# Triangle layer: normalising the input and filling the first channel quarter in one interleaved loop instead of two loops one after the other

## The chip, the cores and the metric

One core of one Trainium2 chip runs the kernel. The metric is the device time of one execution in microseconds (us). The engines are named as the profile names them: PE is the matrix engine, PEld its weight load, DVE the vector engine, ACT the engine of activation functions, POOL the general engine that here scales, shifts and issues stores, and SP the queue that issues loads.

## The reference, cut to what matters

A picture of 256 x 256 pixels with 128 channels goes through four layers, each as `x = x + layer(groupnorm(x))`: attention, a recurrence in the frequency domain, a triangle layer, a convolution. Only the triangle layer is touched. In short, in the reference's own names:

```python
pair_norm = layer_norm(pair, ln_in_w, ln_in_b)          # over the 128 channels of a pixel
p = einsum('bijd,hd->bijh', pair_norm, p_in_w)          # 256 channels out
g = sigmoid(einsum('bijd,hd->bijh', pair_norm, g_in_w))
left, right = g[..., :H] * p[..., :H], g[..., H:] * p[..., H:]
out = einsum('bikd,bjkd->bijd', left, right / L)        # for each channel d a 256x256x256 product
out = einsum('bijh,dh->bijd', layer_norm(out, ...), p_out_w)
return sigmoid(einsum('bijd,ed->bije', pair_norm, g_out_w)) * out
```

`pair` is the group-normalised x, that is x times a factor a plus a shift b for each channel.

## The kernel before, in words

The picture lies in DRAM as 128 channels (partitions) by 65,536 pixels, in 32-bit floats: x2T is the layer's input, znT its normalised input, x3T its output. `triangle` works in these stages:

1. `group_affine` (L1145) turns the statistics of the layer before into the columns `ab` (a and b); `centering` (L136) makes `lc`, the 128 x 128 matrix that takes the channel mean away, scaled by a, and `cb`, the centred b.
2. The norm, a loop over 32 blocks of 2,048 pixels (L1190 to L1235). `load` brings a block into `xin` (a pool of three). `centre` multiplies it by `lc`, two products of 512 pixels for each half block into the PSUM tile `zc`, and DVE adds `cb` into `zs`. `square` is ACT's `sq`. `variance` makes the channel mean of `sq` by four products with a weight 32 columns wide, one for each 512 pixels, which land beside each other on the 128 partitions of one bank; ACT takes `Ln` and `Exp` of it (`rs`). `spreads` brings these rows back to 128 partitions, by four products whose contraction is 32 rows (`pr`). DVE multiplies `zs` by `pr` into `zn`, POOL applies weight and bias in place (L1234) and issues the store to znT (L1235).
3. For each of four channel quarters g: the fill, a loop over 64 half blocks (L1246 to L1257), then the products. The fill loads a block of znT back (`zt`, L1249, the same ring of five buffers that held `zn`), makes eight products with 128 pixels as the weight and the quarter's 128 columns of `wf` as the moving side (`z`), takes `Sigmoid` of one half of the columns (`sg`) and multiplies the other half by it into `LR`, which holds the quarter for the whole picture. The products (`po`, L1259 to L1269) read LR across all pixels: none can start before the quarter's last LR column is written.
4. The output loop (from L1275 on), not touched. It has a mean by narrow products too, `mn`, copied by ACT into `mr` and spread by `spreads`, and it changes ACT's table set twice in each block.

Every engine runs its own instructions in order. Most calls in `triangle` are wrapped in `pin`, which keeps them in the order in which the code issues them on their engine. Before the first block, the loads of `xin` for blocks 0 to 2 have been issued at 2955 to 2962 us, long before `ab` is known at 2997.7 us. ACT's functions come in table sets: the norm uses the set of Ln and Exp, the fill that of Sigmoid, so the set was changed once between the two stages (at 3202.62 us).

Of the kernel before, what the change touches and what calls it, by code (L numbers as in the profile page):

```python
# [9 lines left out]
F32 = mybir.dt.float32  # L10
AF = mybir.ActivationFunctionType
ALU = mybir.AluOpType
AX = mybir.AxisListType
PSUM = bass.MemoryType.PSUM
# [3 lines left out]
P = 128  # L18
# [8 lines left out]
LN_EXP = "natural_log_exp_and_others"  # L27
EXP_TANH = "exp_and_others"
SIGMOID = "sigmoid_and_others"


class Kernel:
# [21 lines left out]
    def act(self, out, in_, func, bias=0.0, scale=1.0, **kw):  # L54
        return self.nc.scalar.activation(out, in_, func, bias=bias, scale=scale, **kw)  # L55

    def table(self, name, key="table"):
        return self.chain(key, self.nc.scalar.preload_act_table_set(name))

    def mm(self, out, lhsT, rhs, start=True, stop=True):  # L60
        return self.nc.tensor.matmul(out, lhsT, rhs, start=start, stop=stop)  # L61
# [1067 lines left out]
    def triangle(self, x2T, x3T, znT, prodD, stats2, shift2, stats3, prepare):  # L1129
# [3 lines left out]
        nc, tc, I = self.nc, self.tc, self.i  # L1133
        V = nc.vector
        NB, G, CQ = NPIX // 1024, 4, P // 4
        pin = lambda f: lambda *a, **k: tc.keep_in_program_order(f(*a, **k))  # L1136
        mm, act, copy = pin(self.mm), pin(self.act), pin(nc.scalar.copy)
        tt, ts, stt, bn = pin(V.tensor_tensor), pin(V.tensor_scalar), pin(V.scalar_tensor_tensor), pin(V.bn_stats)
        table, add = pin(nc.scalar.preload_act_table_set), pin(V.tensor_scalar_add)
        flat = lambda t: t.rearrange("p k n -> p (k n)")  # L1140
        MUL, ADD = ALU.mult, ALU.add
        with ExitStack() as c:
            wp = c.enter_context(self.pool(name="tw", bufs=1))
            with self.pool(name="twp", bufs=2, space=PSUM) as ps0:
                ab = self.group_affine(wp, ps0, stats2, self.g4, "2", shift=shift2, busy=11)  # L1145
                lc, cb = self.centering(wp, ps0, ab, "2")
                W = self.weights
                lnw, lnb, low, lob = (W[n] for n in ("in_w", "in_b", "out_w", "out_b"))
                wpg, oraw, we = W, W["o"], W["e"]
                pb = ps0.tile([P, 2], F32, name="tpbo", tag="gn")  # L1150
                self.mm(pb[:, 0:1], oraw, lob)
                wbo = wp.tile([P, 1], F32, name="twbo")
                V.tensor_copy(wbo, pb[:, 0:1])
                wo = wp.tile([P, P], F32, name="two")
                V.tensor_scalar_mul(wo, oraw, low)

                wf = wp.tile([P, G, 4, CQ], F32, name="wf")
                for n, m in enumerate("gp"):
                    for side in range(2):
                        V.tensor_copy(wf[:, :, 2 * n + side, :],  # L1160
                                      wpg[m][:, side * P:(side + 1) * P].rearrange("c (g d) -> c g d", g=G))
# [7 lines left out]
            V.memset(m32, 1.0 / P)  # L1169
            spread = wp.tile([P, P], F32, name="tspread")  # L1170
            V.memset(spread, 1.0 / 32)

            def variance(ps, work, sq):

                var = ps.tile([P, 512], F32, name="var", tag="r", bufs=2)
                for k in range(4):
                    mm(var[32 * k:32 * k + 32], m32, sq[k // 2][:, (k % 2) * 512:(k % 2 + 1) * 512])
                rs = work.tile([P, 512], F32, name="rs")
                act(rs, var, AF.Ln, bias=self.eps)
                act(rs, rs, AF.Exp, scale=-0.5)  # L1180
                return rs

            def spreads(ps, rs):
                pr = [ps.tile([P, 1024], F32, name="pr", tag="w") for _ in range(2)]
                for k in range(4):
                    mm(pr[k // 2][:, (k % 2) * 512:(k % 2 + 1) * 512], spread[32 * k:32 * k + 32], rs[32 * k:32 * k + 32])
                return pr


            with ExitStack() as c1:  # L1190
                io = c1.enter_context(self.pool(name="t1", bufs=3))
                work = c1.enter_context(self.pool(name="t1w", bufs=4))
                ps = c1.enter_context(self.pool(name="t1s", bufs=3, space=PSUM))
                xin, sq, zs = {}, {}, {}

                def load(m):
                    if m < NB // 2:
                        xin[m] = io.tile([P, 2048], F32, name="xin")
                        nc.sync.dma_start(xin[m], x2T[:, m * 2048:(m + 1) * 2048])

                def centre(m, b):
                    if m >= NB // 2:
                        return
                    zc = ps.tile([P, 1024], F32, name="zc", tag="w")
                    for k in range(2):
                        s = b * 1024 + k * 512
                        mm(zc[:, k * 512:(k + 1) * 512], lc, xin[m][:, s:s + 512])
                    zs[m, b] = work.tile([P, 1024], F32, name="zs")
                    add(zs[m, b], zc, cb)

                def square(m, b):
                    if m < NB // 2:
                        sq[m, b] = work.tile([P, 1024], F32, name="sq")
                        act(sq[m, b], zs[m, b], AF.Square)

                table(LN_EXP)
                for m in range(2):
                    load(m)
                for b in range(2):
                    centre(0, b)  # L1220
                    square(0, b)
                for m in range(NB // 2):
                    load(m + 2)
                    centre(m + 1, 0)
                    rs = variance(ps, work, [sq[m, b] for b in range(2)])
                    square(m + 1, 0)
                    centre(m + 1, 1)
                    square(m + 1, 1)
                    pr = spreads(ps, rs)
                    zn = zp.tile([P, 2048], F32, name="zn", tag="zt")  # L1230
                    for b in range(2):
                        z = zn[:, b * 1024:(b + 1) * 1024]
                        tt(z, zs[m, b], pr[b], MUL)
                        nc.gpsimd.tensor_scalar(z, z, lnw, lnb, MUL, ADD)  # L1234
                    nc.gpsimd.dma_start(znT[:, m * 2048:(m + 1) * 2048], zn)  # L1235

            with ExitStack() as c1:

                LR = c1.enter_context(self.pool(name="tl", bufs=1)).tile([P, 2, 2, 2 * CQ, P], F32, name="LR")
                work = c1.enter_context(self.pool(name="t2w", bufs=2))  # L1240
                io = c1.enter_context(self.pool(name="t2", bufs=3))
                ps = c1.enter_context(self.pool(name="t2s", bufs=2, space=PSUM))
                table(SIGMOID)
                for g in range(G):

                    for b in range(NB):  # L1246
                        if b % 2 == 0:
                            zt = zp.tile([P, 2048], F32, name="zt", tag="zt")
                            nc.sync.dma_start(zt, znT[:, b * 1024:(b + 2) * 1024])  # L1249
                        z = ps.tile([P, 8, P], F32, name="z", bufs=3)  # L1250
                        for ch in range(8):
                            o = (b % 2) * 1024 + ch * P
                            mm(z[:, ch, :], zt[:, o:o + P], wf[:, g].rearrange("c t d -> c (t d)"))
                        sg = work.tile([P, 8, 2 * CQ], F32, name="sg")
                        act(sg, z[:, :, :2 * CQ], AF.Sigmoid)
                        rows = lambda t: t.rearrange("p (x q) f -> p x q f", x=2)
                        tt(LR[:, :, :, :, 2 * b:2 * b + 2].rearrange("p a k f x -> p x (a k) f"),  # L1257
                           rows(z[:, :, 2 * CQ:]), rows(sg), MUL)

                    for d in range(CQ):  # L1260
                        po = ps.tile([P, 2, 2, P], F32, name="po")
                        for a in range(2):
                            for kc in range(2):
                                mm(po[:, a], LR[:, a, kc, d, :], LR[:, :, kc, CQ + d, :], start=kc == 0, stop=kc == 1)
                        o = io.tile([P, 2, P, 2], F32, name="o")
                        for a in range(2):
                            act(o[:, a], po[:, a].rearrange("p b j -> p j b"), AF.Copy, scale=1.0 / N)
                        nc.gpsimd.dma_start(prodD[g * CQ + d].rearrange("(p a j) -> p a j", p=P, a=2),  # L1268
                                            o.rearrange("p a j b -> p a (j b)"))  # L1269
# [5 lines left out]
            with ExitStack() as c1:  # L1275
# [3 lines left out]
                M = NB // 2  # L1279
# [370 lines left out]
```

## Time and profile before

| what | value |
| --- | --- |
| median of three runs | 4823.47 us (4823.44 to 4824.69) |
| profiled execution, its own time | 4823.77 us |
| its span | 4821.7 us |
| PE busy over the span | 96% |
| DVE, ACT, POOL busy over the span | 75%, 68%, 42% |
| norm stage, 2998.66 to 3205.17 us | 206.5 us |
| first quarter's fill, 3205.17 to 3324.28 us | 119.1 us |
| first quarter's products, 3324.28 to 3379.80 us | 55.5 us |
| granted PE clock | 0.99 |

The span runs from the first instruction to the last; 2.1 us of the execution's own time lie around it. Times in the text count from the span's start. A row of the timeline gives start, length, engine, line, operation, the tile written and the tiles read, the shape, how many instructions of the kind follow each other, and in brackets the idle time of the engine before it with what ended it. Each 32-bit matmul of the program shows as two instructions, so `x8` is four products. Lengths reach from the start of an instruction to its end; consecutive instructions of an engine overlap by a little, so the distance between two starts is what an engine can repeat.

### The profile page before, as it was taken

To read this page: it belongs to the slowest core of one execution; us is meant where nothing else is said; L and a number is where in the kernel's file an instruction comes from. 1 tells how busy PE (TensorE), PEld (TensorE's weight loads), DVE (VectorE), ACT (ScalarE), POOL (GpSimd) and SP (SyncE) were. 2 spreads that over 40 slices of the span, in tenths; PEclk is the share of its full clock that TensorE was granted. 3 is DMA by queue.
4 is the path that set the end of the run, shared out by engine and by line. 5 is a ranking of instruction groups with operands and counts; after the bars stand their busy time and mean duration, and the time that the engine had idled before them with its cause. 6 is when DMAs were issued, how large, how long until landed. Compare 5 with 4: busy or idle time off the path is not lost.

```text
span 4821.7 us, 78838 instructions
## 1 busy us (share of the span) xinstructions
PE 4634.6 (96%) x30671; PEld 2636.5 (55%) x30671; DVE 3635.7 (75%) x4553; ACT 3288.8 (68%) x4978; POOL 2007.2 (42%) x1356
## 2 busy tenths in 40 slices
PE   8999999999999899999999997999999999999999
PEld 2444555555555433333333332259999943369999
DVE  6676777777777699999999996763533448899886
ACT  6456888888888799999999996543333357752110
POOL 0343555555555366666676664421011024420000
PEclk9999999999999999999999998999999999999999
DMA  8893122222222245555555555996866779954432
GB/s 302 311 350 116 49 84 88 81 84 89 82 83 88 80 101 132 133 132 129 133 133 133 130 134 128 331 329 237 282 226 224 239 299 386 368 216 162 134 120 71
DMA packets 221172, 835.17 MB, mean 173 GB/s; under 512 B 59158, under 2 KB 62508, under 8 KB 172260
## 3 DMA queue, kind: packets, MB, share of 16 engines
q1 hardware_dynamic: 144622, 498.19, 30.4%
q0 software_dynamic: 74880, 331.50, 23.7%
q8 instruction: 246, 4.03, 0.3%
q14 instruction: 128, 1.05, 0.1%
q10 hardware_dynamic: 1296, 0.40, 0.0%
HBM read 497.84 MB, written 265.03 MB: 158 GB/s over the span
## 4 chain that ended last, share of the span: by engine, by line
PE 66%; ACT 15%; DVE 11%; issue 6%; DMA 2%; POOL 1%; SPq 0%; ACTq 0%; DVEq 0%; POOLq 0%
PE z L61 10%; PE m L61 8%; PE nd L61 7%; PE sc L61 6%; PE zc L61 5%; PE po L61 5%; PE ppq L61 3%; PE ppv L61 3%; PE pe L61 2%; PE py L61 2%; PE ppg L61 2%; PE ppk L61 2%; PE px L61 2%; PE var L61 2%; ACT L950 2%
## 5 line engine op out<-in xcount | busy, mean ns | idle before, releaser
L609 DVE TENSOR_TENSOR e<-sc,bT 128x1024 f32<-128x1024 f32 x512 | 613.4, 1219 | 255.9 <-PE sc L61 253.8
L609 POOL TENSOR_TENSOR ks<-e 128x1024 f32<-128x1024 f32 x256 | 601.6, 2367 | 442.5 <-PE nd L61 429.0
L55 ACT ACTIVATE e<-e 128x1024 f32<-128x1024 f32 x512 | 539.7, 1054 | 39.6 <-DVE e L609 29.9
L1136 DVE TENSOR_TENSOR LR<-z,sg 128x512 f32<-128x512 f32 x256 | 268.4, 1048 | 364.4 <-ACT sg L55 364.4
L61 PE MATMUL m<-U,v 128*128 128x128 f32 x4608 | 514.7, 275 | 0.0
L61 PEld LDWEIGHTS m<-U,v 128*128 128x128 f32 x4608 | 514.6, 192 | 0.0
L61 PE MATMUL z<-wf,zt 128*128 128x128 f32 x4096 | 460.9, 276 | 1.4 <-DVE zn L1136 1.4
L61 PEld LDWEIGHTS z<-wf,zt 128*128 128x128 f32 x4096 | 460.7, 193 | 2.4 <-DVE zn L1136 2.2
L55 ACT ACTIVATE sg<-z 128x512 f32<-128x512 f32 x256 | 152.8, 597 | 309.1 <-PE z L61 309.1
L1268 POOL DMA_DIRECT2D prodD<-o x128 | 69.0, 540 | 618.7 <-ACT o L55 608.8
L61 PE MATMUL sc<-proj 32*128 32x256 f32 x4096 | 300.4, 403 | 2.8 <-DVE e L609 1.9
L978 POOL TENSOR_TENSOR fs<-f 128x512 f32<-128x512 f32 x64 | 175.7, 2745 | 270.6 <-DVE f L975 251.0
L61 PEld LDWEIGHTS sc<-proj 32*128 32x128 f32 x4096 | 188.3, 185 | 160.7 <-PE px L61 94.8
L61 PE MATMUL nd<-e,proj 128*32 128x256 f32 x4096 | 272.1, 383 | 2.6 <-DVE og L609 2.6
L55 ACT ACTIVATE dn<-dn 128x512 f32<-128x512 f32 x384 | 237.9, 620 | 10.1 <-DVE dn L609 6.0
L978 POOL TENSOR_TENSOR u<-t,tr 128x512 f32<-128x512 f32 x64 | 235.3, 3676 | 11.1 <-DVE tr L981 10.0
L1136 POOL TENSOR_TENSOR xin<-ga,xin 128x1024 f32<-128x1024 f32 x62 | 145.5, 2363 | 210.2 <-DVE ga L1136 210.2
L978 POOL TENSOR_TENSOR t<-t,v 128x1024 f32<-128x1024 f32 x64 | 209.6, 3275 | 54.4 <-DVE t L975 54.4
L61 PE MATMUL po<-LR 128*128 128x256 f32 x1024 | 222.1, 379 | 6.9 <-DVE LR L1136 6.9
L1526 ACT COPY m4s<-m 128x512 f32<-128x512 f32 x32 | 18.7, 584 | 289.9 <-PE m L61 289.9
L1536 POOL DMA_DIRECT2D out_dram<-ys x32 | 37.0, 1155 | 425.4 <-DVE ys L1534 425.4
L61 PEld LDWEIGHTS po<-LR 128*128 128x128 f32 x1024 | 194.2, 190 | 34.0 <-DVE LR L1136 7.7
(385 smaller groups left out, 10713.1 us busy)
## 6 DMA issues: line engine op xcount, KB each, us to landing
zt<-znT SPq DMA_DIRECT2D x128, 1024.0 KB
xin<-x2T SPq DMA_DIRECT2D x64, 1024.0 KB
znT<-zn POOLq DMA_DIRECT2D x61, 1024.0 KB, 5.2
xin<-in_x_dram SPq DMA_DIRECT2D x48, 1024.0 KB
xr<-x3T SPq DMA_DIRECT2D x46, 768.0 KB
x1T<-x POOLq DMA_DIRECT2D x64, 512.0 KB, 4.9
xf<-x1T SPq DMA_DIRECT2D x64, 512.0 KB
xc<-x1T SPq DMA_DIRECT2D x128, 256.0 KB
```

Of the source, the lines that this page charges most:

```text
L55: return self.nc.scalar.activation(out, in_, func, bias=bias, scale=scale, **kw)
L61: return self.nc.tensor.matmul(out, lhsT, rhs, start=start, stop=stop)
L609: pin = lambda f: lambda *a, **k: tc.keep_in_program_order(f(*a, **k))
L950: pin(nc.scalar.preload_act_table_set(want))
L978: pin(nc.gpsimd.tensor_tensor(out, a, b_, op))
L1136: pin = lambda f: lambda *a, **k: tc.keep_in_program_order(f(*a, **k))
L1268: nc.gpsimd.dma_start(prodD[g * CQ + d].rearrange("(p a j) -> p a j", p=P, a=2), o.rearrange("p a j b -> p a (j b)"))
L1526: nc.scalar.copy(m4, m[4])
L1536: nc.gpsimd.dma_start(out[row:row + 8].rearrange("r p t c -> p (r t) c"), ys.rearrange("p g k t c -> p (g k t) c"))
```

## The change

The norm of all 32 blocks and the fill of quarter 0 become one loop, written as a list of steps with a lag each: in iteration `it` a step with lag l works on block it - l. One tile per block holds the input, then the centred input, then the normalised input (in place, in the ring of five). The mean is no longer taken away by `lc`: a weight 32 columns wide, `m32a`, which is 1/128 times a, makes the mean of a x as `mn`; ACT copies it to `mr`; `spreads` brings it to 128 partitions (`mb`); DVE makes a x minus mean in one instruction (`zs`). `cb` moves into ACT's `Square` as its bias and into DVE's `(x + cb) * pr` (`zn`). The fill reads the tile straight after POOL's weight and bias; quarter 0 reads nothing of znT back. znT is still stored, since quarters 1 to 3 and the output loop read it. The fill works on 512 pixels at a time in one bank (`z`, a ring of two), instead of on 1,024 in two banks (a ring of three). Mean and variance share a ring of two banks, both kinds of spread rows share a ring of two pairs of banks; `mr`, `sq` and `rs` have one buffer each. `tabled` changes ACT's table set wherever the next step needs another. LR's buffer is taken before the loop.

```diff
-                lc, cb = self.centering(wp, ps0, ab, "2")
+                pc = ps0.tile([P, 2], F32, name="pc2", tag="gn")
+                self.mm(pc[:, 0:1], self.cmat, ab[:, 1:2])
+                cb = wp.tile([P, 1], F32, name="cb2")
+                V.tensor_copy(cb, pc[:, 0:1])
...
+            m32a = wp.tile([P, 32], F32, name="tmeana")
+            V.tensor_scalar_mul(m32a, m32, ab[:, 0:1])
...
-                for m in range(NB // 2):
-                    load(m + 2)
-                    centre(m + 1, 0)
-                    rs = variance(ps, work, [sq[m, b] for b in range(2)])
-                    square(m + 1, 0)
-                    centre(m + 1, 1)
-                    square(m + 1, 1)
-                    pr = spreads(ps, rs)
-                    zn = zp.tile([P, 2048], F32, name="zn", tag="zt")
-                    for b in range(2):
-                        z = zn[:, b * 1024:(b + 1) * 1024]
-                        tt(z, zs[m, b], pr[b], MUL)
-                        nc.gpsimd.tensor_scalar(z, z, lnw, lnb, MUL, ADD)
-                    nc.gpsimd.dma_start(znT[:, m * 2048:(m + 1) * 2048], zn)
...
+                    work = c2.enter_context(self.pool(name="t1w", bufs=1))
+                    ps = c2.enter_context(self.pool(name="t1s", bufs=2, space=PSUM))
...
+                    def tabled(name, *a, **k):
+                        if loaded[0] != name:
+                            table(name)
+                            loaded[0] = name
+                        act(*a, **k)
+
+                    def four(d, name, w, srcs):
+                        d[name] = ps.tile([P, 512], F32, name=name, tag="r")
+                        for k in range(4):
+                            mm(d[name][32 * k:32 * k + 32], w, srcs[k])
...
+                    def ld(d):
+                        d["x"] = zp.tile([P, 2048], F32, name="zn", tag="zt")
+                        nc.sync.dma_start(d["x"], x2T[:, d["p"] * 2048:(d["p"] + 1) * 2048])
+                    def mn(d): four(d, "mn", m32a, [chunk(d["x"], k) for k in range(4)])
+                    def mc(d):
+                        d["mr"] = work.tile([P, 512], F32, name="mr")
+                        act(d["mr"], d["mn"], AF.Copy)
+                    def mb(d): d["mb"] = spreads(ps, d["mr"])
+                    def zs(d):
+                        for h in range(2):
+                            stt(half(d["x"], h), half(d["x"], h), ab[:, 0:1], d["mb"][h], MUL, ALU.subtract)
+                    def sq(d):
+                        d["sq"] = work.tile([P, 2048], F32, name="sq")
+                        for h in range(2):
+                            act(half(d["sq"], h), half(d["x"], h), AF.Square, bias=cb)
+                    def vr(d): four(d, "vr", m32, [chunk(d["sq"], k) for k in range(4)])
+                    def rs(d):
+                        d["rs"] = work.tile([P, 512], F32, name="rs")
+                        tabled(LN_EXP, d["rs"], d["vr"], AF.Ln, bias=self.eps)
+                        act(d["rs"], d["rs"], AF.Exp, scale=-0.5)
+                    def pr(d): d["pr"] = spreads(ps, d["rs"])
+                    def zn(d):
+                        for h in range(2):
+                            stt(half(d["x"], h), half(d["x"], h), cb, d["pr"][h], ADD, MUL)
+                    def af(d):
+                        for h in range(2):
+                            pin(nc.gpsimd.tensor_scalar)(half(d["x"], h), half(d["x"], h), lnw, lnb, MUL, ADD)
+                    def sto(d): pin(nc.gpsimd.dma_start)(znT[:, d["p"] * 2048:(d["p"] + 1) * 2048], d["x"])
+                    def fill(k):
+                        def f(d):
+                            d["z", k] = ps.tile([P, 4, P], F32, name="z", tag="z")
+                            for ch in range(4):
+                                o = k * 512 + ch * P
+                                mm(d["z", k][:, ch, :], d["x"][:, o:o + P], wf[:, 0].rearrange("c t d -> c (t d)"))
+                        def s(d):
+                            d["g", k] = work.tile([P, 4, 2 * CQ], F32, name="sg", bufs=2)
+                            tabled(SIGMOID, d["g", k], d["z", k][:, :, :2 * CQ], AF.Sigmoid)
+                        def t(d):
+                            tt(LR[:, :, :, :, 4 * d["p"] + k].rearrange("p a k f -> p (a k) f"), d["z", k][:, :, 2 * CQ:], d["g", k], MUL)
+                        return f, s, t
+                    (f0, s0, t0), (f1, s1, t1), (f2, s2, t2), (f3, s3, t3) = (fill(k) for k in range(4))
+                    order = (
+                     (ld, 0), (mn, 0), (pr, 2), (zn, 2), (af, 2), (f3, 3), (f1, 3), (mc, 0), (s3, 3), (t3, 3),
+                     (s1, 3), (vr, 1), (t1, 3), (mb, 0), (f0, 2), (rs, 1), (f2, 2), (s2, 2), (zs, 0), (s0, 2),
+                     (t0, 2), (sq, 0), (sto, 2), (t2, 2),
+                    )
+                    for it in range(M + max(lag for _, lag in order)):
+                        for step, lag in order:
+                            if 0 <= it - lag < M:
+                                D[it - lag]["p"] = it - lag
+                                step(D[it - lag])
...
-                    for b in range(NB):
+                    for b in range(NB if g else 0):
```

More of the change, by code (lines that the diff above doesn't have):

```diff
@@ L1190, in triangle @@
             with ExitStack() as c1:
[L1191 to L1214, printed above, removed]
@@ L1216, in triangle @@
-                table(LN_EXP)
-                for m in range(2):
-                    load(m)
-                for b in range(2):
-                    centre(0, b)
-                    square(0, b)
-                for m in range(NB // 2):
-                    load(m + 2)
-                    centre(m + 1, 0)
-                    rs = variance(ps, work, [sq[m, b] for b in range(2)])
-                    square(m + 1, 0)
-                    centre(m + 1, 1)
-                    square(m + 1, 1)
-                    pr = spreads(ps, rs)
-                    zn = zp.tile([P, 2048], F32, name="zn", tag="zt")
-                    for b in range(2):
-                        z = zn[:, b * 1024:(b + 1) * 1024]
-                        tt(z, zs[m, b], pr[b], MUL)
-                        nc.gpsimd.tensor_scalar(z, z, lnw, lnb, MUL, ADD)
-                    nc.gpsimd.dma_start(znT[:, m * 2048:(m + 1) * 2048], zn)
@@ L1237, in triangle @@
-            with ExitStack() as c1:
-                LR = c1.enter_context(self.pool(name="tl", bufs=1)).tile([P, 2, 2, 2 * CQ, P], F32, name="LR")
+                LR = c1.enter_context(self.pool(name="tl", bufs=1)).tile([P, 2, 2, 2 * CQ, P], F32, name="LR")
+                with ExitStack() as c2:
+                    work = c2.enter_context(self.pool(name="t1w", bufs=1))
+                    ps = c2.enter_context(self.pool(name="t1s", bufs=2, space=PSUM))
+                    M = NB // 2
+                    D = [{} for _ in range(M)]
+                    loaded = [None]
+                    def tabled(name, *a, **k):
[7 more added lines that the diff above has]
+                            mm(d[name][32 * k:32 * k + 32], w, srcs[k])
+                    half = lambda t, h: t[:, h * 1024:(h + 1) * 1024]
+                    chunk = lambda t, k: t[:, k * 512:(k + 1) * 512]
+                    def ld(d):
[49 more added lines that the diff above has]
+                                step(D[it - lag])
```

## The prediction

> **What bounds the kernel now.** First the chain that ended last, near 3200 us (start, length, engine and work):
>
> ```profile
> 3205.17 117.39 PE z L61 x1024
> 3324.28 55.52 PE po L61 x256
> 3379.80 114.36 PE z L61 x1024
> ```
>
> From the first fill on, PE alone carries the end: each fill is one PE run with no gap that matters. The first is 3.0 us longer than the second although it has the same 512 products: PE had just idled and began slowly. Next the busy time by stage, norm and first fill (PE, PEld, DVE, ACT, POOL, each with its count; granted clock; DMA share; GB/s):
>
> ```profile
> 2998.66:3205.20 206.54, 192.34 (x769) 58.84 (x769) 150.81 (x128) 107.62 (x129) 90.90 (x93) 1.00 0.86 314
> 3205.20:3324.30 119.10, 117.36 (x1025) 117.17 (x1025) 68.19 (x65) 38.21 (x64) 2.93 (x3) 0.98 0.89 313
> ```
>
> PE is nearly full in both; ACT is busy for 107.6 and 38.2 us only, DVE for 150.8 and 68.2. The two stages take 3324.28 - 2998.66 = 325.6 us, 10.2 per block of 2,048 pixels. One turn of the norm, from the timeline:
>
> ```profile
> 3083.62 1.14 PE L61 MATMUL pr<-rs,tspread 32*128 32x512 f32 x8
> ...
> 3083.79 1.28 DVE L1136 TENSOR_SCALAR zs<-zc,cb 128x1024 f32<-128x1024 f32 x1 [1.59 <-PE zc L61]
> 3084.99 2.34 DVE L1136 TENSOR_TENSOR zn<-zs,pr 128x1024 f32<-128x1024 f32 x2
> ...
> 3085.13 1.98 PE L61 MATMUL zc<-xin,lc 128*128 128x512 f32 x4 [0.37 <-DVE zs L1136]
> ...
> 3089.95 1.14 PE L61 MATMUL pr<-rs,tspread 32*128 32x512 f32 x8
> ```
>
> It repeats every 6.33 us. Of that `zc` is 3.63 us of PE (the chain gives eight instructions 3.63), and the rest is hand-overs PE - DVE - PE as well as work. Last, the output loop, which already does what the new loop will do:
>
> ```profile
> 4045.26 1.28 ACT L1136 ACT_TABLE_LOAD   x1
> ...
> 4045.50 1.14 PE L61 MATMUL pr<-rs,tspread 32*128 32x512 f32 x8
> ...
> 4046.57 1.07 PE L61 MATMUL var<-sq,tmean 128*32 128x512 f32 x8
> ...
> 4047.45 1.04 PE L61 MATMUL mn<-pr,tmean 128*32 128x512 f32 x8
> ...
> 4047.71 0.69 ACT L55 ACTIVATE rs<-var,eps 128x512 f32<-128x512 f32 x1 [1.16 <-PE var L61]
> ...
> 4048.43 3.70 PE L61 MATMUL pe<-zn,w2e 128*128 128x512 f32 x8
> ...
> 4049.56 1.28 ACT L1136 ACT_TABLE_LOAD   x1
> ...
> 4050.86 1.02 ACT L55 ACTIVATE ga<-pe 128x1024 f32<-128x1024 f32 x1
> ```
>
> Distances of starts give what repeats: spread 1.07, narrow group 0.88 and 0.98, table load to next activation 1.30.
>
> **What the skill says.** "TensorEngine Tiling (Array Packing)", Tiling Modes: weights of 32 columns or contractions of 32 rows split the array in four tiles that work at once, and a change of mode drains the array. The trace agrees: a narrow group of four products takes 0.9 us of PE where the same moving data cost `zc` 3.63, and the drain is the 0.1 between 0.88 and 0.98. "ScalarE: Activation LUTs", What ACT_TABLE_LOAD costs: 1.283 us plus a drain of 1.380. Here the load is 1.28 and the next activation starts at 1.30; no second part is seen. "TensorE: Matmul & The Clock Gate", Part 1: after an idle window of about 3.4 us PE runs at half speed for as long. The 3.0 us lost at 3205 fits.
>
> **The change part by part, for one block in steady state.**
>
> PE loses `zc` (3.63), gains `mn` and `mb`: two narrow groups at 0.93 (1.86), two spreads at 1.07 (2.14), sixteen fill products at 114.36/512 = 0.223 (3.57). Sum 7.57 us.
>
> ACT, by distances of starts: `mr` 0.48 (128x512 out of PSUM at 2804.40 to 2804.88); four `sg` of 128x256, for which `o<-po` of that shape stands: a pair takes 0.66, one 0.38, so three at 0.28 and the one ahead of a load at 0.38, 1.22; two table loads at 1.30, 2.60; Ln 0.72 (from its start to that of Exp, 4048.43); Exp its whole 0.63, as a load follows; two squares at 0.95 (128x1024 at 2812.22 to 2813.16), each with 0.05 for the bias (the same 128x512 step takes 0.57 with one, 0.52 without), 2.00. Sum 7.65 us. The built order confirms two loads in every iteration, 60-odd in place of two.
>
> DVE: `zs` and `zn`, four instructions of 128x1024. This mix of operands, SBUF, a column and PSUM, isn't in the trace; `ga<-py,twbo,ga` (the same operation with PSUM first) takes 1.28 and `zn<-zs,pr` 1.21, starts 1.14 to 1.20 apart; I take 1.20. Four `t` of 128x256 at half of LR's 1.05, 0.52, since its strided writes made it cost by the element; up to 0.70 would put DVE level with the others. Sum 6.9. POOL: 2.37 + 0.56 = 2.9, hidden.
>
> So two engines want 7.6 us each. A turn with in-order queues and single buffers can't, by these sums, fall below 7.65, and each hand-over costs a little: `mb` waits for DVE's `zn` (its ring has one pair for each use), behind it on PE are the fill products f0 and f2, and for those wait `sg` and `t`; `f3` waits for DVE's `t0` of the turn before. I take 7.9, with 7.5 to 8.8 as bounds.
>
> Loads: a buffer of five comes free when f1 has read it, about 3.8 us into iteration b-2, and the next tenant is wanted at the start of iteration b: 2 x 7.9 - 3.8 = 12.0 us to land. Landings of `xin` took 4.1 to 12.0 us, median 10.0; in this stage the load issued at 3064.73 was down at 3071.1. Traffic is 2 MB per 7.9 us where it was 2 MB per 6.33. It fits, narrowly at the worst landing. The store has three turns: issued some 6 us into b-3, 5.2 us to land.
>
> The start: the first block's load no longer goes out at 2955.75. In the built program it waits, counted by PE's semaphore, for the recurrence's last products (`partps`, 2990.39), since its buffer overlies them; blocks 1 and 2 wait for the last stores to x2T, issued at 2986.92. SP is behind them in order. With 6.5 us to land, block 0 is there at about 2997.3; the loop starts at 2998.66 as before (it waits for `twbo`). Margin 1.3 us; I charge nothing. Blocks 1 and 2 follow 3 us apart and are wanted later.
>
> The head: `mn`, `mr`, `mb` 2.8 us; then `mb`, `zs`, squares, `vr`, next `mb` 5.8; then two tables' worth, Ln, Exp, `pr`, f0 and f2 9.2: 17.8 us to the fourth `mn`. Then 28 turns. After the last `mn`: one turn, then 7.4, 7.0 and 3.0 as steps drop out. PE idles by microseconds in the head, so a half-speed start like that at 3205 is charged once, 3.0. Stage = 17.8 + 28T + T + 17.4 + 3.0 = 38.2 + 29T; with T = 7.9, 267.3 us.
>
> Nothing for: `lc` replaced by the smaller `tmeana`, beside the `pc` product; the 32 loads of znT that quarter 0 drops, since its PE run never waited for one; the Sigmoid reload after the loop, 1.28 us of ACT under the first two `po` tiles (3.5 us of PE), which need no copy before the third.
>
> Saving 325.6 - 267.3 = 58.3 of the profiled execution's 4823.77 gives 4765.5; the median is 0.3 lower: 4765.
>
> **The rivals.** (a) PE alone sets the turn, ACT and DVE hide: T 7.5, no cold start, 252.7 us, 4750.5. For it: ACT's sum uses ends where a start might do. Against: the sums are equal within 0.1. (b) Waits couple the three queues: T 8.5, 284.7 us, 4783; a late load of 14 us gives T = 8.9 and 4795. For it: one buffer each for `mr`, `sq`, `rs`, and DVE 87% full between two full engines. Against: lags of one to three turns leave most waits already met. (c) Slower: each table switch costs the page's 2.66 us, drain included. Then ACT is 7.65 + 2 x 1.36 = 10.4, the stage 339.8, the time 4838. It decides from T = (325.6 - 38.2)/29 = 9.9, a switch of 2.4 us. For it: every switch follows live work. Against: the two rows above at 1.30, next to live work too. Products that don't run at once would cost more still, but `mn` and `var` above exclude it.
>
> **How the numbers follow.** T from 7.65 to 8.2, 4757 to 4774: 0.55. Case (a) with T below that: 0.12. Case (b), 4774 to 4795: 0.25. Between there and break-even: 0.04. Slower: 0.03, and 0.01 for within 0.2% (about what can be told from no change), as only T near 9.9 gives it. Eight tenths lie within 4751 to 4791.
>
> **What would show it.** Right: the first `po` at about 3266; turns of 7.7 to 8.2 us between `mn` groups; ACT and PE over 90% busy there, 1.28 us loads with no gap after them; `mn` at 0.9. Wrong: PE waiting at `mn` for a load, DVE's `t` well over 0.55, gaps after table loads, or PE at half speed beyond the head.

## The result, and the profile after

The changed kernel takes 4769.64 us in the median of four runs (4767.09 to 4772.24), the kernel before 4823.45 us. The ratio of the new time to the old is 0.9889, with a 95% interval of 0.9872 to 0.9906: 53.8 us less. The forecast was 4765 us, 58.3 us less. The profiled execution took 4772.24 us with a span of 4770.2, so the two profiled spans differ by 51.5 us, and that is what the traces below have to add up to.

The chain that ended last, near the end of the new loop (start, length, engine and work):

```profile
3242.31 0.99 PE mn L61 x8
3243.30 1.07 PE pr L61 x8
3244.38 1.98 PE z L61 x16
3246.36 0.99 PE vr L61 x8
3247.35 1.07 PE pr L61 x8
3248.42 1.98 PE z L61 x16
```

This is one turn, and all of it is PE: mean, spread of the root, eight fill products, variance, spread of the mean, eight fill products. It adds up to 8.08 us, and 28 turns, from the fourth `mn` at 3015.53 us to the last at 3242.24, take 8.10 us each. Busy time by stage: head, steady turns, tail (PE, PEld, DVE, ACT, POOL, each with its count; granted clock; DMA share; GB/s):

```profile
2998.49:3015.53 17.04, 14.17 (x88) 4.73 (x88) 9.93 (x9) 11.35 (x13) 2.99 (x3) 1.00 0.45 188
3015.53:3242.50 226.97, 226.97 (x1797) 130.68 (x1800) 195.27 (x225) 217.24 (x308) 82.36 (x84) 1.00 0.70 256
3242.50:3270.00 27.50, 22.12 (x169) 15.12 (x162) 18.17 (x25) 18.94 (x31) 8.82 (x9) 1.00 0.76 269
```

In the steady part PE has not one gap: 226.97 us busy of 226.97. (The ends of products are modelled in the profile, so a full row alone doesn't prove that PE sets the turn; experiments 1 and 3 test it.) ACT is busy for 217.24, next in line. One turn of ACT from the timeline, from one change of table set to the same one a turn later:

```profile
3125.35 1.28 ACT L1136 ACT_TABLE_LOAD   x1
...
3126.64 0.69 ACT L55 ACTIVATE rs<-vr,eps 128x512 f32<-128x512 f32 x1
...
3127.36 0.63 ACT L55 ACTIVATE rs<-rs 128x512 f32<-128x512 f32 x1
3128.01 1.28 ACT L1136 ACT_TABLE_LOAD   x1
...
3129.30 0.66 ACT L55 ACTIVATE sg<-z 128x256 f32<-128x256 f32 x2
3129.85 2.19 ACT L55 ACTIVATE sq<-zn,cb 128x1024 f32<-128x1024 f32 x2
...
3131.93 0.59 ACT L55 ACTIVATE mr<-mn 128x512 f32<-128x512 f32 x1
3132.41 0.39 ACT L55 ACTIVATE sg<-z 128x256 f32<-128x256 f32 x1
...
3133.04 0.39 ACT L55 ACTIVATE sg<-z 128x256 f32<-128x256 f32 x1 [0.24 <-PE z L61]
3133.44 1.28 ACT L1136 ACT_TABLE_LOAD   x1
```

The only wait in it is 0.24 us for PE's fill product. A table load is followed within 0.02 us by the next activation.

Where the 51.5 us come from: norm and first fill took 325.6 us before (2998.66 to 3324.28) and take 271.3 us now (2998.49 to 3269.75), 54.4 less, and they start 0.2 us earlier. Two stretches go the other way: the first quarter's products take 1.2 us more (56.7 for 55.5), and everything from the second fill to the end takes 1.8 us more (1443.7 for 1441.9). The 1.8 us lie at the start of the output loop, where PE waits 5.91 us for its first load and waited 3.61 before. In the other runs of the tied loop below this wait is 3.23 us (four buffers) to 6.29 us (more work for ACT), so the change alone doesn't set it; what does stays open. The 1.2 us are a wait in the chain just after the loop:

```profile
3272.74 6.04 DMA prodD<-o
...
3278.88 0.67 ACT o L55 x2
...
3279.59 46.89 PE po L61 x216
```

The first store of a product landed after 6.04 us, while such stores took 2.3 us in the median in the kernel before; ACT waited for its buffer, and PE for ACT.

### The profile page after: what moved, and what is told of

Read it like the earlier page. It is cut to its first block, busy times and chain, and to the rows that moved or that the text cites. A ratio compares the mean times of both kernels' runs of the same rounds, so it can differ in the third digit from the quotient of the medians.

```text
span 4770.2 us, 79683 instructions
## 1 busy us (share of the span) xinstructions
PE 4587.0 (96%) x30927; PEld 2608.0 (55%) x30927; DVE 3641.1 (76%) x4617; ACT 3390.9 (71%) x5135; POOL 2012.0 (42%) x1356
## 3 DMA queue, kind: packets, MB, share of 16 engines
q14 instruction: 130, 1.06, 0.1%
## 4 chain that ended last, share of the span: by engine, by line
PE 65%; ACT 14%; DVE 10%; issue 6%; DMA 2%; POOL 2%; SPq 0%; ACTq 0%; POOLq 0%; DVEq 0%
PE z L61 10%; PE m L61 8%; PE nd L61 7%; PE sc L61 6%; PE po L61 5%; PE pr L61 3%; PE ppq L61 3%; PE ppv L61 3%; PE zc L61 2%; PE pe L61 2%; PE py L61 2%; PE ppg L61 2%; PE ppk L61 2%; PE px L61 2%; ACT L950 2%
## 5 line engine op out<-in xcount | busy, mean ns | idle before, releaser
L1136 DVE TENSOR_TENSOR LR<-z,sg 128x512 f32<-128x512 f32 (+1 forms) x320 | 269.4, 873 | 336.3 <-ACT sg L55 336.3
L61 PEld LDWEIGHTS z<-wf,zt 128*128 128x128 f32 x3072 | 343.5, 192 | 0.2
L61 PE MATMUL z<-wf,zt 128*128 128x128 f32 x3072 | 343.5, 275 | 0.0
L55 ACT ACTIVATE sg<-z 128x512 f32<-128x512 f32 (+1 forms) x320 | 160.6, 512 | 244.6 <-PE z L61 244.3
```

## The experiments

**1. Is it ACT that sets the turn?** The prediction took ACT's 7.65 us and added hand-overs. So take ACT's table loads away.

```diff
-                        tabled(LN_EXP, d["rs"], d["vr"], AF.Ln, bias=self.eps)
-                        act(d["rs"], d["rs"], AF.Exp, scale=-0.5)
+                        act(d["rs"], d["vr"], AF.Identity, bias=self.eps)
+                        act(d["rs"], d["rs"], AF.Square, scale=-0.5)
```

> Ln and Exp are replaced by Identity and Square of the same shapes, which need no table set, so the loop changes no table; the root isn't computed. It leaves 2.6 us of ACT out of each turn. If PE with its mode changes sets the turn: it stays at 8.09 us and the time at 4767 to 4772. If ACT and the hand-overs set it, as the prediction had it: the turn falls to PE's 7.6, 29 turns x 0.5 = 14 us less, about 4755.

Measured: 4769.81 us, ratio 0.9888 (0.9871 to 0.9904), and a turn of 8.10 us. From its timeline:

```profile
3120.43 0.66 ACT L55 ACTIVATE sg<-z 128x256 f32<-128x256 f32 x2 [1.67 <-PE z L61]
...
3124.48 0.38 ACT L55 ACTIVATE sg<-z 128x256 f32<-128x256 f32 x1 [0.51 <-PE z L61]
...
3128.53 0.66 ACT L55 ACTIVATE sg<-z 128x256 f32<-128x256 f32 x2 [1.67 <-PE z L61]
```

The time taken from ACT came back as waits for PE. As long as PE sets the turn, two table loads in every turn cost this kernel nothing.

**2. How much slack has ACT?** A first try asked for one more table load in each turn.

```diff
+                        table(LN_EXP)
                         tabled(LN_EXP, d["rs"], d["vr"], AF.Ln, bias=self.eps)
```

> One more load of a table set in each turn, 1.28 us of ACT. If PE sets the turn and ACT has only the 0.2 to 0.3 us of slack that its busy time shows (217.2 of 227.0 us), ACT takes over at about 7.8 + 1.3 = 9.1 us, 29 turns x 1.0 = 29 us more, about 4799. If ACT sets the turn already: 9.4 us, 38 us more, 4807. If ACT has over 1.3 us of slack: nothing, 4770.

It measured 4767.21 us (ratio 0.9887, 0.9871 to 0.9904), and the profile shows two loads in each turn, as in the change: a load of the set that is already active never reached the chip. So it says nothing on slack and stands as a repetition of the change. In this repetition the first products ran their 55.5 us with no wait for a store, so the 1.2 us above don't belong to every execution.

The second try does half of each square twice.

```diff
-                            act(half(d["sq"], h), half(d["x"], h), AF.Square, bias=cb)
+                            for _ in range(2 - h):
+                                act(half(d["sq"], h), half(d["x"], h), AF.Square, bias=cb)
```

> The first half of each square is done twice, about 1.0 us more of ACT in each turn; PE's and DVE's work stays. The second result is the same as the first. ACT is busy for 217.2 us of 227.0 in the change's steady turns, 7.75 us of each 8.09, so it has at most 0.35 us of slack: the turn becomes 7.75 + 1.0 = 8.75 us, 29 x 0.66 = 19 us more, about 4789. If the engines are so loosely tied that ACT could still hide it: 4770. If ACT's work is on PE's path by hand-overs: the full 1.0 us, 4799.

One run: 4797.67 us. In the steady turns the chain that ended last now holds ACT alone; the end of one turn of it, and then the same turn from the timeline:

```profile
3127.28 1.13 ACT sq L55
3128.42 0.48 ACT mr L55
3128.90 0.55 ACT sg L55 x2
3129.45 0.02 issue
3129.46 1.28 ACT L1136
```

```profile
3120.54 1.28 ACT L1136 ACT_TABLE_LOAD   x1
...
3125.05 3.37 ACT L55 ACTIVATE sq<-zn,cb 128x1024 f32<-128x1024 f32 x3
3128.32 0.57 ACT L55 ACTIVATE mr<-mn 128x512 f32<-128x512 f32 x1
...
3129.46 1.28 ACT L1136 ACT_TABLE_LOAD   x1
```

The turn is 8.92 us (3120.54 to 3129.46). From the first square to `mr` it holds 3.27 us (3125.05 to 3128.32), where the change has 2.08 (3129.85 to 3131.93): the added square costs 1.19. It is more than the 1.04 between two squares of the change: the repeated square writes the same half tile as the first, and starts at 3126.23 us, after the first has ended at 3126.20. Without it ACT needs 8.92 - 1.19 = 7.73 us. So ACT's slack in the change is 8.10 - 7.73 = 0.37 us a turn: PE sets the turn, but a PE made faster would gain 29 x 0.37 = 11 us at most before ACT stops it. (The time is 8.7 us above what was expected for this case; 29 x 0.82 by the measured turn gives 24 of the 28 us over the change.)

**3. What in PE was undersized?** The prediction's sum for PE was 7.57 us. PE works in three modes here: 32 columns at a time for the means, 32 rows for the spreads, the full array for the fill, and a turn changes mode six times. Two runs have the same added work, a second group for the mean. In one it follows the first directly; in the other it stands between two fill products, which adds two changes.

```diff
+                    def mn2(d):
+                        for k in range(4):
+                            mm(d["mn"][32 * k:32 * k + 32], m32a, chunk(d["x"], k))
...
-                     (ld, 0), (mn, 0), (pr, 2), (zn, 2), (af, 2), (f3, 3), (f1, 3), (mc, 0), (s3, 3), (t3, 3),
+                     (ld, 0), (mn, 0), (mn2, 0), (pr, 2), (zn, 2), (af, 2), (f3, 3), (f1, 3), (mc, 0), (s3, 3), (t3, 3),
```

> The four narrow products of the mean are done twice, one group right after the other in the same mode, so no mode change is added. If PE sets the turn: 8.09 + 0.87 = 8.96 us, 29 x 0.87 = 25 us more than the change, about 4795. If ACT or hand-overs set it: less than 10 us more.

```diff
-                     (ld, 0), (mn, 0), (pr, 2), (zn, 2), (af, 2), (f3, 3), (f1, 3), (mc, 0), (s3, 3), (t3, 3),
+                     (ld, 0), (mn, 0), (pr, 2), (zn, 2), (af, 2), (f3, 3), (mn2, 0), (f1, 3), (mc, 0), (s3, 3), (t3, 3),
```

> The same second group of the mean, but put between the fill products f3 and f1, so that the work is that of the doubled mean and two mode changes are added. If a change costs 0.175 us: the turn is 0.35 us longer than with the doubled mean, 9.31 us, 10 us more in the time, about 4805. If changes are free and the 0.2 us are hand-overs: as with the doubled mean, 4795.

Measured: 4793.50 us (ratio 0.9935, 0.9918 to 0.9952) with turns of 8.95 to 8.96 us, and 4804.66 us (0.9959, 0.9945 to 0.9974) with turns of 9.28 to 9.29. First the doubled, then the split one, from their timelines:

```profile
3121.58 1.92 PE L61 MATMUL mn<-zn,tmeana 128*32 128x512 f32 x16
...
3123.44 1.14 PE L61 MATMUL pr<-rs,tspread 32*128 32x512 f32 x8
```

```profile
3126.02 1.07 PE L61 MATMUL mn<-zn,tmeana 128*32 128x512 f32 x8
...
3127.02 1.14 PE L61 MATMUL pr<-rs,tspread 32*128 32x512 f32 x8
3128.09 1.16 PE L61 MATMUL z<-wf,zn 128*128 128x128 f32 x8
3129.18 1.07 PE L61 MATMUL mn<-zn,tmeana 128*32 128x512 f32 x8
```

A second group in the same mode adds 0.86 us (8.96 - 8.10), so every microsecond put on PE shows in the turn. Two more changes of mode add 0.33 (9.29 - 8.96), 0.17 us each, with the same products in both runs. If all six cost that, they are 1.0 us of the turn's 8.10. Bare, a narrow group is 0.87 us and eight fill products 1.79; with 0.87 for a bare spread too, 4 x 0.87 + 2 x 1.79 = 7.06, and 7.06 + 6 x 0.17 = 8.08. The two runs price the changes between the narrow and the full mode. For the changes to and from the spreads, and for a bare spread, there is this sum alone.

**4. Which half of the change brings the gain?** First the tie alone, with the mean taken away by the full matrix as before.

```diff
-                    def mb(d): d["mb"] = spreads(ps, d["mr"])
+                    def mb(d):
+                        d["mb"] = [ps.tile([P, 1024], F32, name="zc", tag="w") for _ in range(2)]
+                        for k in range(4):
+                            mm(d["mb"][k // 2][:, (k % 2) * 512:(k % 2 + 1) * 512], lc, chunk(d["x"], k))
...
-                            stt(half(d["x"], h), half(d["x"], h), ab[:, 0:1], d["mb"][h], MUL, ALU.subtract)
+                            pin(V.tensor_copy)(half(d["x"], h), d["mb"][h])
...
-                     (ld, 0), (mn, 0), (pr, 2), (zn, 2), (af, 2), (f3, 3), (f1, 3), (mc, 0), (s3, 3), (t3, 3),
+                     (ld, 0), (pr, 2), (zn, 2), (af, 2), (f3, 3), (f1, 3), (s3, 3), (t3, 3),
```

> The loop stays tied, but the mean is taken away by the full 128x128 matrix as before (four products of 512 pixels into two pairs of banks, DVE copies them into the tile) and the two narrow groups mn and mb and the copy mr go. If PE sets the turn: pr 0.87 + vr 0.87 + 3.62 + fill 3.57 + four mode changes at 0.175 = 9.63 us, 29 x 1.54 = 45 us more than the change, about 4814, so nearly the whole gain is the narrow products'. If the tie is the gain: 4770 to 4780.

Measured: 4822.03 us, ratio 0.9994 (0.9985 to 1.0002), a turn of 9.85 us. From its timeline:

```profile
3122.17 1.14 PE L61 MATMUL pr<-rs,tspread 32*128 32x512 f32 x8
...
3123.63 2.05 PE L61 MATMUL z<-wf,zn 128*128 128x128 f32 x16 [0.33 <-DVE LR L1136]
...
3125.61 1.06 PE L61 MATMUL vr<-sq,tmean 128*32 128x512 f32 x8
...
3126.61 3.70 PE L61 MATMUL zc<-zn,lc 128*128 128x512 f32 x8
```

PE is the bound again: its work takes 9.85 - 0.33 = 9.52 us of the turn (9.63 were expected), and one wait of 0.33 us for DVE comes on top. Tying the stages together, by itself, brings nothing that can be measured.

Then the narrow products alone: the same steps without the fill for all blocks, then the fill from znT as before. The spread rows get the two banks that the fill doesn't use.

```diff
-                    ps = c2.enter_context(self.pool(name="t1s", bufs=2, space=PSUM))
+                    ps = c2.enter_context(self.pool(name="t1s", bufs=3, space=PSUM))
...
-                        d[name] = ps.tile([P, 512], F32, name=name, tag="r")
+                        d[name] = ps.tile([P, 512], F32, name=name, tag="r", bufs=2)
...
+                     (ld, 0), (mn, 0), (pr, 2), (zn, 2), (af, 2), (mc, 0), (vr, 1), (mb, 0), (rs, 1), (zs, 0),
+                     (sq, 0), (sto, 2),
...
-                    for b in range(NB if g else 0):
+                    for b in range(NB):
```

> The narrow products in place, but not tied: the same steps without the fill for all blocks, then quarter 0 filled from znT like the others; the spread rows get a ring of three pairs of banks, since the fill's two banks are free. If engines set the norm's turn (DVE 4.8, PE 4.1 us with changes): 5.0 to 5.5 us, norm 165 to 180 us, time about 4785 to 4800. If memory traffic sets it (2 MB a turn, before at 331 GB/s in 6.33 us): 6.0 to 6.3 us, norm about 200 to 205 us, time 4815 to 4824, and the tie is what brings the gain.

Measured: 4832.44 us, ratio 1.0019 (1.0012 to 1.0026): slower than before by 0.2%, and outside both expectations. Its turns are uneven, 5.07 to 10.2 us from one `vr` to the next, 6.5 in the mean. A late one from the chain and from the timeline, and the row of the waits:

```profile
3067.39 8.00 DMA znT<-zn
...
3075.45 7.07 DMA zn<-x2T
...
3082.57 1.93 PE mn L61 x8
```

```profile
3082.57 1.93 PE L61 MATMUL mn<-zn,tmeana 128*32 128x512 f32 x8 [3.00 <-DMA zn<-x2T]
```

```profile
PEld mn L61 <- DMA zn<-x2T: 40.0, 16, 4.5
```

PE waits for loads of the block tile, up to 4.5 us at a time. In the chain a load starts only when the store that holds its tile has landed: 8.00 and 7.07 us, one behind the other. The wait also costs more than its own length: after it the group `mn` takes 1.93 us, where it takes 1.06 in an even turn, and over the norm the granted clock is 0.93. To test what makes the loads late, the store to znT was left out of this version (the fills and the output loop then read x2T, so that nothing unwritten is read).

```diff
                      (ld, 0), (mn, 0), (pr, 2), (zn, 2), (af, 2), (mc, 0), (vr, 1), (mb, 0), (rs, 1), (zs, 0),
-                     (sq, 0), (sto, 2),
+                     (sq, 0),
...
-                            nc.sync.dma_start(zt, znT[:, b * 1024:(b + 2) * 1024])
+                            nc.sync.dma_start(zt, x2T[:, b * 1024:(b + 2) * 1024])
```

> As the untied version, but the norm's store to znT is left out, and the fills and the output loop read x2T where they read znT, so the traffic of the norm is halved. If memory traffic set the untied norm's turn: it falls to DVE's 4.8 to 5.3 us. If engines set it: it stays as in the untied version, within 0.1 us.

One run: 4804.69 us, where the kernel before took 4825.29 beside it, with turns of 5.92 us and no wait for a load. This is neither of the two expectations. What waits now is PE's weight load for `vr`, for ACT's squares (us in total over the norm, times, longest):

```profile
PEld vr L61 <- ACT sq L55: 63.3, 64, 2.5
```

So the 5.92 us hold waits of PE for ACT, in this order of the steps; another order was not tried. Leaving the store out removes its traffic, but a store also holds its tile, so it frees the tiles earlier too. The last run tells these apart: the store is there, and the norm has ten tiles of its own.

```diff
-                        d["x"] = zp.tile([P, 2048], F32, name="zn", tag="zt")
+                        d["x"] = work.tile([P, 2048], F32, name="zn", bufs=10)
...
-                LR = c1.enter_context(self.pool(name="tl", bufs=1)).tile([P, 2, 2, 2 * CQ, P], F32, name="LR")
                 with ExitStack() as c2:
...
+                LR = c1.enter_context(self.pool(name="tl", bufs=1)).tile([P, 2, 2, 2 * CQ, P], F32, name="LR")
                 work = c1.enter_context(self.pool(name="t2w", bufs=2))
```

> As the untied version with its store, but the norm's tiles come from a ring of ten buffers of their own (LR is taken after the loop, which leaves the room), so that a store or a load under way holds no tile that the loop wants. If the untied version's waits for loads came from the ring of five: the turn falls to the 5.92 us seen without the store, the norm to about 194 us and the time to about 4811. If they came from memory traffic: the turns stay uneven with a mean of 6.4 to 6.6 us, and the time is 4825 to 4833.

Measured: 4832.27 us, ratio 1.0019 (1.0011 to 1.0027). The turn and the time disagree with each other, and the timeline says why:

```profile
3013.83 1.06 PE L61 MATMUL mn<-zn,tmeana 128*32 128x512 f32 x8
...
3182.10 1.06 PE L61 MATMUL mn<-zn,tmeana 128*32 128x512 f32 x8
3188.03 1.06 PE L61 MATMUL mn<-zn,tmeana 128*32 128x512 f32 x8
```

The turns are even, 5.92 us, with the full traffic, which in places ran at 430 GB/s. So the untied version's waits came from the ring of five, which the input, the store and the norm share: it has too few tiles for loads and stores as long as those above, while the memory carries the traffic of a 5.92 us turn. But in this run the stage before ends late, for a reason that was not followed up, and the first `mn` comes at 3013.83 us instead of 2999.98; and after the norm the first column of LR, which here is taken only after the loop, waits for the last store to land, 8.61 us in the chain. So the time doesn't move. Even without these two, 5.92 for 6.33 us would be 13 us in 32 blocks.

Taken together: the tie alone changes nothing beyond the noise, the narrow products alone cost 9 us, and both together gain 53.8. About 6 of the 9 us are the turns, 6.51 us in the mean for 6.33, which the late loads lengthen. What the narrow products alone could gain at best, with enough tiles and another order of their steps, was not measured.

**5. Is the ring of five just enough?** The same ring in the tied loop, with four buffers.

```diff
-            zp = quarters.enter_context(self.pool(name="tz", bufs=5))
+            zp = quarters.enter_context(self.pool(name="tz", bufs=4))
```

> The ring of block tiles has four buffers, not five. By the prediction's rule a tile's next load can go out 3.8 us into the iteration before the one that wants it: one turn has to hold 3.8 us and the landing. With a landing of 6.4 us the turn is 10.2 us, 29 x 2.1 = 61 us more, about 4831; with 10 us it is 13.8 us and about 4935. If loads have plenty of room: 8.09 us, 4770.

One run: 4800.67 us, with turns of 8.9 to 9.3 us for the most part:

```profile
3123.38 1.06 PE L61 MATMUL mn<-zn,tmeana 128*32 128x512 f32 x8 [0.75 <-DMA zn<-x2T]
```

And the load for the next `mn`, from the chain:

```profile
3127.56 4.95 DMA zn<-x2T
...
3132.56 1.07 PE mn L61 x8
```

PE now waits at `mn` in nearly every turn, as the prediction's rule for a late load had it. The rule's form holds and its landing time was too long: a turn of 9.1 us less the 4.0 us until f1 has read the tile (0.99 + 1.07 + 1.98) leaves 5.1 us for a load, not 6.4 or more, and the chain shows 4.95. With five buffers there were 8.1 + 4.1 = 12.2 us for it, so five is more than enough here and four is just too few.

## Why the prediction was right, and where it wasn't

The range and the sign held, and the forecast is 5 us off. Most of the sum was right as it stood; its reason for the turn was not. That the number came so close is in part luck: ACT's sum and the hand-overs, which don't set the turn, raised it from PE's 7.57 to 7.9 us, where the mode changes that were left out raise it to 8.10; and outside the turn the errors partly cancel.

- **What sets the turn.** The step "a turn … can't, by these sums, fall below 7.65, and each hand-over costs a little" is what failed: it put the bound on ACT's sum and 0.25 us on hand-overs. There are no hand-overs on the path. PE is busy without a gap, taking 2.6 us of work out of ACT changes nothing, and work put on PE shows one for one. The turn is 8.10, not 7.9, which over 28 turns is 5.5 us, the whole of the miss and a little more.
- **PE's sum of 7.57 us** was undersized by 0.5. The output loop's distances that it took, 0.93 as a mean for narrow groups and 1.07 for spreads, hold part of the mode changes; narrow groups measure 0.99, spreads 1.07, and eight fill products 1.98, where 114.36/512 of an unbroken fill gave 1.79. That the array drains on a change of mode, which the Trainium skill states in "TensorEngine Tiling (Array Packing)", Tiling Modes, was quoted and read as 0.1 us, from one row. Here a change costs 0.17 us. Of the 1.0 us for six of them the sum held about half, and the fill products' share, 2 x 0.19 us, not at all.
- **ACT's sum of 7.65 us** measures 7.73: it was sized well, with 0.08 missing on the two squares (2.08 for 2.00). The table loads were sized well too (1.28, next start 0.02 us later): the drain of 1.38 us that the Trainium skill gives in "ScalarE: Activation LUTs", What ACT_TABLE_LOAD costs, doesn't show in this loop either, so the slower rival (c) falls. Rival (a), a turn of PE's 7.5 us, was right that PE alone sets it and falls for PE's price. Rival (b), coupled waits, falls too: in the steady turns every wait is off the path.
- **DVE's** `zs` and `zn`, of a kind that the trace before didn't show, take 1.28 us with starts 1.19 apart (1.20 assumed), the 128x256 `t` 0.53 (0.52 assumed).
- **Head and tail.** The head took 17.0 us (17.8 expected). The tail, from the last `mn` to the first `po`, took 27.5 us where a turn of 7.9 and 17.4 made 25.3: PE waits 1.36, 1.27 and 1.37 us for DVE's `LR` before the last three groups of fill products. That the ring of two banks makes it wait was not tested. Together with the 3.0 us below: -0.8 - 3.0 + 2.2 + 5.5 = 3.9 us over the 267.3, and 271.3 was measured.
- **The start.** The first load went out at 2991.62 us and the first `mn` ran at 2998.49, without a wait for it.
- **What was priced at nothing.** Neither the dropped loads nor the Sigmoid reload shows in the chain, as said. Missed was the products' first store, which landed late: 1.2 us in the profiled execution, none in its repetition. What held it up was not tested.
- **The 3.0 us for a half-speed PE** weren't needed: the clock is 1.00 in all three parts. The reading behind them was too simple. In the kernel before, the first 6.8 us of the fill look like this (the columns as above):

```profile
3205.20:3208.60 3.40, 3.40 (x16) 3.40 (x17) 1.04 (x1) 0.00 (x0) 2.93 (x3) 0.50 0.95 383
3208.60:3212.00 3.40, 3.40 (x22) 3.40 (x22) 1.03 (x1) 0.79 (x2) 0.00 (x0) 0.65 1.03 359
```

A clock of 0.50 and then of 0.65 is half speed for about 5.8 us, not for the 3.4 that the prediction took, and that is the loss of about 3.0. Nor was there one long idle stretch ahead of it: PE's gaps were 0.47, 1.45 and 1.37 us. The head of the new loop has gaps of 0.72, 1.60 and 0.46 us at full clock. What decides between the two, these traces don't show.

## What to carry to other kernels

Count PE's changes of tiling mode as work, 0.17 us each here, and take the price of a group from a place where it stands between the same neighbours. A change made of two parts can be worth nothing in either part as it stands and a lot together: the narrow products made room on PE, and the tie is what filled it. In steady turns a block takes 6.33 + 3.57 = 9.9 us before (turn of the norm and its share of an unbroken fill), 9.85 tied with the wide mean, 5.92 + 3.57 = 9.5 untied where no tile is waited for, and 8.1 with both. When an engine is full to the last tenth, ask what the next one needs: here ACT stands 0.37 us behind, so the six mode changes can't be turned into more than about 11 us. And when work is added to measure slack, read from the trace what it cost there, which was 1.19 us for a square of 1.04.

## What the hardware showed that I had not expected

A change of PE's mode is paid on both sides: in the steady turns the first fill product after a spread takes 0.38 us for 0.28, and the narrow group after a fill starts 0.2 us after the last product, where products follow each other at 0.11. A load of the table set that is already active cost nothing, as it wasn't run. Memory traffic of 430 GB/s was carried in the untied norm with ten tiles (410 over 90 us at a DMA share of 1.00), over a third above the 314 of the norm before at a share of 0.86.
